# Moving one folded weight pair ahead of a branch, and its successor's loads behind a fetch

## The chip, the cores and the metric

The kernel runs on one core of one Trainium2 chip. The metric is the device time of one execution in microseconds (us). Three runs of the kernel before took 694.87, 694.79 and 693.70 us; their median is 694.79 us. Smaller is better. A separate execution was recorded by the hardware profiler; it took 693.57 us, and the span from its first to its last instruction, which all times below are counted from, is 691.8 us long.

The core has five engines that run their own instruction streams and wait for each other through semaphores: TensorE (PE in the profile, with weight loads shown apart as PEld), VectorE (DVE), ScalarE (ACT), GpSimd (POOL), and SyncE (SP), which here does nothing but start transfers.

## The reference, cut to what matters

The model is two transformer blocks on 800 tokens (8 sequences of 100) of width 512, all in float32:

```
x = x + attention0(layernorm(x), ctx[:, :100])     # 16 heads, causal
x = x + experts(layernorm(x))                      # 8 experts, 2 per token
x = x + attention1(layernorm(x), ctx)              # 16 latent heads over 361 rows
x = x + quantised_ffn(layernorm(x))                # 512 -> 2 x 1408 -> 512, int8-like rounding
```

Two parts touch the change. The first is the routing of the second line:

```
scores = x @ Wg.T ; topk_s, topk_i = top_k(scores, 2) ; probs = softmax(topk_s)
y += w[..., e] * (silu(x @ W1[e].T) * (x @ W2[e].T)) @ W3[e]     for each of 8 experts
```

The second is in the third line, where the queries of a head h pass through three weights one after the other:

```
q_hk = hidden_q @ Wq.T ; q_big = q_hk . w_kc_q[h] ; q_r = q_big . W_qr[h]
```

The product of those three weights doesn't depend on the data, so the kernel computes it once, two heads at a time, and multiplies the tokens with the result. That is called folding below, and two heads are a pair. There are eight pairs, 0 to 7.

## The kernel before, in words

The kernel goes through the four lines in order. Tokens are tiled in seven tiles of 128 rows (the last has 32). Each expert gets 240 slots in a DRAM buffer, `x_slot`: the routing computes for each token the slots of its two experts, and 14 indirect transfers started by POOL (line 680) scatter the normalised rows there. Expert e then fetches its 240 rows (`fetch`, line 960), turns them into columns by 8 transposes (`columns_of`, line 985; the two copies out of PSUM are lines 989 on ACT and 987 on DVE), and multiplies (`products`, line 1053).

**The branch.** Should an expert get more than 240 tokens, a slow path handles the rest. DVE computes a flag, `spilt` (line 806), PE, DVE, ACT and POOL each read it into a register (line 879), and all branch on it (line 886). The slow path isn't taken with these inputs, so each engine jumps over it. The rows of expert 0 can't be fetched before the scatters have landed, so around the branch PE has little else to do than folding.

**Folding a pair** takes a chain across two engines:

- `fold_head` (line 705): for each of the two heads three matmuls of 64 columns on PE; `fold_copy` (line 713): ACT copies the result to `a_p`. The two are `fold_first`.
- `fold_second` (line 723): two matmuls of 512 columns on PE, each on half of the array's columns; ACT copies the result to `f_p` (line 727).
- `fold_third` (line 733): four transposes on PE; ACT copies them into `wqf` (line 734), which the second attention reads much later.

A float32 matmul appears in the profile as two records, so the six matmuls of line 705 are x12 there.

A pair's weights are loaded by `fold_load` (lines 694, 698 and 699): five transfers started by SP, 1,088 KB together, into one of three buffers. Pairs 0 to 2 are loaded early. Pair 0 is folded ahead of the branch. Pairs 3 to 7 are folded one per expert, in experts 0 to 4, between the products of that expert (lines 1085, 1091 and 1103).

**The order of the work.** PE, DVE and ACT follow the order in which the code is written inside `tc.manual_schedule` regions; there is one up to line 868 and another from line 1035. Between them, and for SP's transfers, the framework's scheduler decides. `tc.issue_after` (line 1023) holds the transfers written behind it until the rows of expert 1 have been asked for. In the built program the first part of pair 1 stands wholly ahead of the branch on PE and ACT, both heads and the copy to `a_p`, although line 1037 is written behind it. Behind the branch stand, on PE, in this order: line 705 of pair 2, line 723 of pair 1, line 723 of pair 2, line 733 of pair 1, line 733 of pair 2, the transposes of expert 0's rows (line 985), and expert 0's products. On ACT stand a load of an activation table, `a_p` of pair 2, `f_p` of pairs 1 and 2, `wqf` of pairs 1 and 2, the rows' copy (line 989), and then the load of the table that holds Silu (line 1064). SP starts pair 3's five transfers ahead of the branch, and behind it the rows of experts 0 and 1, three tiles of `gu` (a weight of the last line that is quantised on the side, line 823), one of `dn` (line 828), and pair 4's five transfers.

## Time and profile before

| | |
|---|---|
| median of three runs | 694.79 us (693.70 to 694.87) |
| the profiled execution | 693.57 us, span 691.8 us |
| mean granted clock of TensorE over the span | 0.976 of full speed |
| PE busy | 651.2 us, 94% of the span |
| DVE, ACT, POOL busy | 419.9, 245.3, 183.6 us |
| longest idle time of PE around the branch | 8.12 us, until 136.12 us |
| expert 0's first product on PE | 145.71 us |
| last scatter started by POOL | 134.22 us |
| expert 0's rows asked for by SP | from 137.05 us |

How to read it: a row of an engine's timeline gives start, duration, engine, line and operation, with the tiles written and read, the number of records merged into it and, in brackets, how long that engine sat idle before it and what released it. The chain of work that ended last is followed back from the last instruction, so what stands on it set the end. PEclk is the share of full clock that the chip granted TensorE in a stretch. Idle time of an engine that isn't on the chain costs nothing.

### The profile page before, as it was taken

The numbers are of one execution on the slowest core, as the hardware profiler recorded it, in microseconds if no ns is written. First come the engines' busy times: TensorE is split into PE (matmuls) and PEld (weight loads), VectorE is DVE, ScalarE is ACT, GpSimd is POOL, SyncE is SP. The second block draws the span as 40 slices with busy tenths as digits, with TensorE's granted clock in tenths as the row PEclk, the third lists the DMA queues.
The fourth block names the chain that finished last, engine by engine and source line by source line (L and its number), as shares of the span: only waits on it lengthen the run. The fifth ranks groups of instructions, "written<-read, shape, count | busy, mean of one in ns | idle before, by whom it ended". The sixth has DMA issues, their size and how long they took to land.

```text
span 691.8 us, 10209 instructions
## 1 busy us (share of the span) xinstructions
PE 651.2 (94%) x3637; PEld 420.4 (61%) x3637; DVE 419.9 (61%) x1059; ACT 245.3 (35%) x557; POOL 183.6 (27%) x197
## 2 busy tenths in 40 slices
PE   8999997499999999996899999999999999999995
PEld 6767755466776677475676666666666644444442
DVE  4775688326666452442347867876666356566687
ACT  3554454141122111330135555555555412221140
POOL 2132231601111111168114233233333202211021
PEclk9999999589999999999799999999999999999999
DMA  8700293699999997744010210210000030111211
GB/s 296 236 17 18 95 328 114 238 306 260 308 275 311 315 254 186 191 137 133 15 16 1 57 42 16 57 34 11 2 12 1 3 125 8 29 28 29 48 35 63
DMA packets 80313, 80.41 MB, mean 116 GB/s; under 512 B 41284, under 2 KB 54136, under 8 KB 80128
## 3 DMA queue, kind: packets, MB, share of 16 engines
q1 hardware_dynamic: 76543, 70.97, 35.6%
q0 software_dynamic: 3712, 8.72, 5.6%
q8 instruction: 30, 0.49, 0.3%
q14 instruction: 28, 0.22, 0.1%
HBM read 56.36 MB, written 16.50 MB: 105 GB/s over the span
## 4 chain that ended last, share of the span: by engine, by line
PE 65%; DVE 7%; DMA 2%; POOL 2%; issue 2%; ACT 1%; SPq 1%; ACTq 0%; POOLq 0%; DVEq 0%
PE bank L357 11%; PE bank L1053 11%; PE bank L1330 10%; PE bank L1310 7%; PE bank L1267 6%; PE bank L1117 6%; PE bank L1324 4%; PE bank L1453 3%; POOL e L1318 2%; PE bank L1300 2%; PE bank L705 1%; DVE nm L1312 1%; PE bank L723 1%; PE bank L985 1%; DMA sin_sb<-in_rope_sin 1%
## 5 line engine op out<-in xcount | busy, mean ns | idle before, releaser
L1318 POOL TENSOR_SCALAR e<-e,rs 128x361 f32<-128x361 f32 (+1 forms) x56 | 66.9, 1196 | 146.4 <-DVE rs L1317 143.2
L357 PE MATMUL bank<-wvo,ctxT 128*128 128x512 f32 x192 | 83.9, 593 | 0.0
L1310 PE MATMUL bank<-kvT,qe 128*128 128x361 f32 (+1 forms) x208 | 82.0, 477 | 0.0
L1053 PE MATMUL bank<-xgT,w 128*128 128x240 f32 (+1 forms) x384 | 76.4, 370 | 0.9 <-ACT xgT L989 0.9
L1053 PEld LDWEIGHTS bank<-xgT,w 128*128 128x128 f32 (+1 forms) x384 | 63.9, 181 | 15.5 <-issue 9.9
L1330 PE MATMUL bank<-pT,kvr 121*128 121x400 f32 x192 | 70.4, 502 | 1.8 <-DVE pT L80 1.8
L1315 ACT ACTIVATE e<-bank,nm 128x361 f32<-128x361 f32 (+1 forms) x104 | 58.8, 565 | 31.3 <-DVE nm L1312 22.4
L1312 DVE TENSOR_REDUCE nm<-bank 128x1 f32<-128x361 f32 (+1 forms) x104 | 54.9, 528 | 21.5 <-PE bank L1310 20.4
L1324 PEld LDWEIGHTS bank<-ident,e 128*121 128x121 f32 (+1 forms) x312 | 47.3, 183 | 33.7 <-POOL e L1318 7.3
L357 PEld LDWEIGHTS bank<-wvo,ctxT 128*128 128x128 f32 x192 | 36.2, 190 | 43.1 <-issue 42.6
L1128 POOL DMA_INDIRECT x_acc<-y,place x16 | 24.4, 1526 | 125.4 <-ACT y L1127 122.1
L1324 PE MATMUL bank<-ident,e 128*121 128x128 f32 (+1 forms) x312 | 52.7, 279 | 2.1 <-POOL e L1318 2.1
L1470 POOL TENSOR_TENSOR hid<-g,u 128x512 f32<-128x512 f32 (+1 forms) x17 | 20.5, 1215 | 111.1 <-ACT g L1461 74.8
L1330 PEld LDWEIGHTS bank<-pT,kvr 121*128 121x128 f32 x192 | 33.9, 190 | 21.4 <-issue 2.0
L1267 PE MATMUL bank<-xT,wqf 128*128 128x256 f32 (+1 forms) x192 | 45.5, 399 | 0.7 <-ACT xT L1252 0.7
L322 POOL TENSOR_TENSOR s<-s,rs 100x800 f32<-100x800 f32 x16 | 24.4, 1523 | 72.4 <-DVE rs L321 30.5
L1117 PE MATMUL bank<-w,hT 128*128 128x512 f32 (+3 forms) x96 | 43.0, 596 | 0.3 <-DVE hT L1077 0.3
L1267 PEld LDWEIGHTS bank<-xT,wqf 128*128 128x128 f32 x192 | 37.4, 196 | 7.9 <-ACT xT L1252 0.9
L1310 PEld LDWEIGHTS bank<-kvT,qe 128*128 128x128 f32 (+1 forms) x208 | 32.5, 186 | 9.4
L82 ACT COPY pT<-bank 121x384 f32<-121x384 f32 (+1 forms) x51 | 23.8, 466 | 32.1 <-PE bank L1324 31.5
L80 DVE COPY ctxT<-bank 128x400 f32<-128x400 f32 (+2 forms) x23 | 13.1, 573 | 32.3 <-PE bank L1267 22.9
L1065 DVE TENSOR_TENSOR hT<-silu,bank 128x240 f32<-128x240 f32 x16 | 6.5, 404 | 39.5 <-ACT silu L1064 39.5
(251 smaller groups left out, 1034.6 us busy)
## 6 DMA issues: line engine op xcount, KB each, us to landing
w<-in_w SPq DMA_DIRECT2D x8, 1408.0 KB
gu<-in_wgu SPq DMA_DIRECT2D x22, 256.0 KB
w<-in_w SPq DMA_DIRECT2D x16, 256.0 KB
wq_p<-in_wq SPq DMA_DIRECT2D x8, 512.0 KB
wo<-in_wo SPq DMA_DIRECT2D x8, 512.0 KB
x_slot<-zeros SPq DMA_DIRECT2D x1, 3840.0 KB
kq_p<-in_wkcq SPq DMA_DIRECT2D x16, 192.0 KB
dn<-in_wdn SPq DMA_DIRECT2D x4, 704.0 KB
```

What stands on the lines that cost most here:

```text
L322: nc.gpsimd.tensor_tensor(part, part, rs.unsqueeze(2).to_broadcast([S, 8, S]), ALU.mult)
L357: nc.tensor.matmul(po[:, :D], lhs[:, c, ds(t * P, r)], rhs[:, c, :], start=(c == 0), stop=(c == chunks - 1),)
L1053: nc.tensor.matmul(po, w12_e[:, c, cols], xgT[:, c, :], start=(c == c0), stop=(c == c1 - 1))
L1117: nc.tensor.matmul(py[i][:n], hT[:mr, m, ds(s0, n)], w3_e[:mr, m, :], start=(m == 0), stop=(m == 2))
L1128: d = nc.gpsimd.indirect_dma_start(out=x_acc, out_offset=bass.IndirectOffsetOnAxis(ap=place[:, 0:1], axis=0), in_=y, in_offset=None, compu ...
L1267: nc.tensor.matmul(pq[:, i, :], wqf[:, c, ts(p0 + i, P)], xT[:, c, :], start=(c == 0), stop=(c == KC - 1),)
L1310: nc.tensor.matmul(ps[:r, :L], qe[:, ds(k0, r)], kvT, start=True, stop=True)
L1312: nc.vector.tensor_reduce(nm[:r], ps[:r, :L], AX.X, ALU.max, negate=True)
L1315: nc.scalar.activation(e[:r], ps[:r, :L], AF.Exp, bias=nm[:r], accum_out=sm[:r])
L1318: (nc.vector if odd else nc.gpsimd).tensor_scalar_mul(e[:r], e[:r], rs[:r])
L1324: nc.tensor.transpose(pt[:LP, c, :r], e[:r, ds(c * (LP - 1), LP)], ident[:r, :r])
L1330: nc.tensor.matmul(pc[:, :VC], kvr[:, c, :], pT[:, c, ts(j, VC)], start=(c == 0), stop=(c == LC - 1))
```

## The change

Four edits, all around the branch:

- Pair 1 is folded whole in the part written ahead of the branch: `fold_second` and `fold_third` of it now stand behind the matmuls that count each expert's tokens (line 800).
- Behind the branch only pair 2 is folded, step by step.
- A one-element Silu on ACT is written at the head of the second ordered region, so that the table with Silu is loaded there.
- Pair 3's loads move from ahead of the branch to behind the rows of experts 0 and 1, ahead of the `gu` tiles.

```diff
     part = fold_second(*part)
-    loaded.append(fold_load(pairs_left.pop(0)))
     xT = gate_columns(5, 7)
     fold_third(*part)
     gate_scores(5, 7, xT)
 
-    loads = loaded.pop(0)
-    pa = fold_head(*loads, 0)
+    part = fold_first(*loaded.pop(0))
     rank_choices(5, 7)
     give_slots(5, 7)
...
     spilt = gp.tile([P, 1], I32, tag="spilt", name="spilt")
     nc.vector.tensor_scalar(spilt, most, float(CAP), None, ALU.is_gt)
+    part = fold_second(*part)
+    fold_third(*part)
     close_atw()
...
     behind_slots = tc.issue_after(slots[1][-1][1])
     behind_slots.__enter__()
+    loaded.append(fold_load(pairs_left.pop(0)))
     gate_up_in = [load_gate_up(gate_up_left.pop(0)) for _ in range(GB)]
...
-    part = fold_copy(*loads, fold_head(*loads, 1, pa))
-    following = fold_first(*loaded.pop(0))
+    nc.scalar.activation(most, ln_eps, AF.Silu)
+    part = fold_first(*loaded.pop(0))
     part = fold_second(*part)
-    following = fold_second(*following)
     fold_third(*part)
-    fold_third(*following)
     turned = columns_of(0, slots[0])
```

In the built program the engines' orders change as follows. PE: line 723 and line 733 of pair 1 (six instructions) move from behind the branch to right ahead of PE's read of the flag. ACT: `f_p` and `wqf` of pair 1 move ahead of the branch too, and the scheduler puts the table load and the one-element Silu there as well, between them and ACT's read of the flag; the two table loads behind the branch are gone. DVE and POOL: no change of order. SP: pair 3's five transfers as said; expert 2's first weight load (line 483) now stands behind two transposing transfers and two loads that it stood ahead of, and the loads of the weights for the second attention (lines 1015 and 1018) stand later.

## The prediction

> **What bounds the kernel now.** I read the page first, then the chain of work that ended last around the branch, then the timelines of PE, ACT and SP there, and last a table of stretches. The page gives the span and the clock in 40 slices of 17.3 us:

> ```profile
> span 691.8 us, 10209 instructions
> ...
> PEclk9999999589999999999799999999999999999999
> ```

> PE is 94% busy, so time is lost only where PE waits or is slow. There are two dips of the clock; the first, in slices 7 and 8 (121 to 156 us), is where the change is. The chain of work from 126 to 150 us (start, duration, what):

> ```profile
> 131.97 4.14 issue
> 136.12 2.79 PE bank L705 x12
> 138.91 3.69 PE bank L723 x8
> ...
> 142.68 0.59 ACT f_p L727
> ...
> 144.57 0.59 ACT xgT L989
> ...
> 145.71 3.48 PE bank L1053 x16
> ```

> Behind the branch the end is set by PE's own folding, not by the rows: those of expert 0 landed at 139.68 and 141.31 us (completions of their semaphores), the transposes of line 985 start at 143.81. From 145.71 PE works through expert 0 without a gap. The change is worth what it moves that 145.71, and what it does to PE's speed behind it. ACT's timeline there:

> ```profile
> 138.99 1.28 ACT L713 ACT_TABLE_LOAD   x1 [11.32 <-PE bank L705]
> 140.28 0.27 ACT L713 COPY a_p<-bank 128x128 f32<-128x128 f32 x1
> 140.86 0.59 ACT L727 COPY f_p<-bank 128x512 f32<-128x512 f32 x1 [0.31 <-PE bank L723]
> ```

> The 1.28 us table load delays `a_p` of pair 2, but meanwhile PE runs line 723 of pair 1 (138.84 to 140.82): hidden. The stretches are cut where I found the clock to change (PE busy, PEld, DVE, ACT, POOL, PEclk, DMA share, GB/s):

> ```profile
> 2.69:6.11 3.42, 2.16 (x5) 0.78 (x4) 1.78 (x5) 0.29 (x1) 2.06 (x25) 1.00 0.91 270
> ...
> 118.74:122.16 3.42, 1.39 (x11) 1.11 (x12) 2.09 (x6) 2.68 (x5) 2.58 (x3) 1.00 0.81 218
> 122.16:125.57 3.41, 3.00 (x21) 2.07 (x19) 0.89 (x6) 0.94 (x3) 2.50 (x4) 0.50 1.05 375
> ...
> 135.81:139.23 3.42, 3.12 (x14) 2.93 (x16) 0.00 (x0) 0.24 (x1) 0.00 (x0) 0.50 0.36 92
> 139.23:142.64 3.41, 3.41 (x9) 0.43 (x6) 0.00 (x0) 1.90 (x3) 0.00 (x0) 0.50 0.97 268
> 142.64:146.05 3.41, 2.38 (x18) 1.95 (x19) 1.03 (x5) 3.18 (x5) 0.00 (x0) 1.00 1.01 374
> ...
> 333.78:337.20 3.42, 3.42 (x10) 2.75 (x9) 0.62 (x2) 0.29 (x2) 0.00 (x0) 0.50 0.02 5
> ```

> The clock falls to half at 122.16 and comes back at 142.64, after a stretch that PE filled with the four 512-wide matmuls of line 723. The stretch before, 91% busy with the 64-wide matmuls of line 705, didn't bring it back.

> [...] 122.16, 142.64, 326.96 and 337.20 are 6.0, 54.0 and 3.0 windows apart. [...] Here windows of 3.41 us out of 3.41 released it (139.23, 333.78, 6.11), windows of 3.12 and 3.00 didn't, nor did that from 2.69 with 2.16 (the 1.00 in its row is only the absence of an earlier record; its four matmuls of 384 columns take 2.93 us, half speed). [...] PE's second branch record takes 3.785 us (132.06 to 135.84).

> **The change part by part**, against the profiled execution (693.57 us, span 691.8), phase of the windows as there.

> *Pair 1 ahead of the branch.* It runs in PE's gap of 8.12 us, at half clock. Line 723 from 128.00, 1.98 us as measured behind the branch: 129.98. `f_p` 0.59 plus 0.05: 130.62. Line 733 from 130.70, about 1.1 us (four such transposes at half clock took 1.09 at 328.98): 131.8. PE's read of the flag stands behind it in order and could start at 130.54 before. It now has to follow the issue of line 733, some 0.45 us later; if the sequencer runs ahead of that wait, 0, at most 1.2 (to the end of line 733). I take 0.45, since PE also waits for its own last instruction (131.91 before) ahead of the jump. So PE comes out at 136.57 instead of 136.12: +0.45. POOL's scatters, DVE's flag and SP's fetch (137.05, released by the last scatter) don't wait for any of it.

> *Table load and Silu.* On ACT: `wqf` 131.9 to 132.5, table 1.28, the one element 0.2: 134.05. ACT waits for its own last instruction, then jumps. With PE's 3.8 us it is back at 137.9, before it is needed at 139.4 (end of line 705). Before, it jumped at 131.5 and gave no sign of life until 138.94, so its jump may take up to 7.4 us; that bound would cost 2.1 us. I take 0. The table load at 145.17, also taken away, was hidden by the first products (Silu at 149.23): 0.

> *Behind the branch, one pair.* Now nothing lies between the steps. Line 705: 136.57 + 2.79 = 139.36. `a_p` 0.27 and two hand-overs of 0.05: line 723 from 139.74, 1.98, to 141.72. `f_p`: line 733 from 142.42. The 1.98 and 0.66 us of pair 1 are gone from the chain, but PE stands still for 0.38 and 0.70 us, since no second pair fills those waits.

> *What that does to the clock.* The window 139.23 to 142.64 now holds 0.13 us of line 705, 1.98 of line 723 and 0.22 of line 733: 2.33 of 3.41, 68%, against 100%. The windows known to fail had 63% (from 2.69; 51% without transposes), 88% and 91%. So I take it that the clock doesn't come back. Then line 733 takes 1.1 (to 143.5), line 985 twice 0.98 (to 145.45), the second half's copy 0.2 + 0.62 as before (to 146.3), and the first product starts at 146.4: 0.7 later than 145.71. The window to 146.05 is transposes; the next, 146.05 to 149.47, is full of products, and releases the clock at 149.47. Until then a product record takes about 0.40 instead of 0.2175 us (3.48 for 16, times 1.83, as line 723's four records took 1.08 at full clock, at 117.25, and 1.98 at half): 3.07 us do the work of 1.67, a loss of 1.40. Sum: **+2.1 us**. If the window grid lies otherwise, the release comes up to one window later: another 3.41 x 0.456 = 1.6.

> *Pair 3's loads.* Five transfers, 1,088 KB. Pair 4's five took 3.9 us (147.6 to 151.5, semaphores). So everything behind them on SP's queue lands 3.9 us later, `gu` at 148.4 to 149.8 instead of 144.56 to 145.86, `dn` at 151.5 instead of 147.6. DVE takes the first `gu` at 149.95 and `dn` at 154.5: hidden, by 1.5 us at the least. Pair 3 itself lands at 147.4 and is wanted by PE at 149.0 (later with a slow clock): hidden by 1.6. If late, a us for each us. Expert 2's weights, asked for at 157.6, now wait for DVE's second `gu` (about 162); 1,408 KB at some 300 GB/s is 5 us more, needed at 182.3: hidden by over 10. The transfers removed from 116.9 to 119.9 freed bandwidth for the scatters, but POOL starts these 1.27 us apart and SP waits for the last start: 0.

> Sum +2.1 us on 693.57; the median of the runs shown is 1.2 above that execution, and I carry the difference over: 694.79 + 2.1 = 696.9 us. From no change this kernel's measurement can tell about 0.2%, 1.4 us.

> **The rivals.**
> *The clock comes back within the single pair's chain.* If a window needs only some 60% of matmuls, 142.64 stays the moment of release. Then line 733 ends at 143.2, line 985 at 144.2, the copy at 145.0, first product at 145.1: -0.6, so 694.2. It decides at a threshold under 68%; for: no window between 63% and 88% is in the trace; against: those of 88% and 91% failed, if on narrow matmuls. This one ends not slower.
> *The clock was late before, too, in most runs.* Only 3.74 us of line 723 stand there, a window is 3.41; if it must lie wholly inside, that happens for a tenth of the phases. Then the median of before is a slow-clock run: its first product comes at 147.4 (two pairs at half clock), after's at 146.4: -1.0 or, with an earlier window, up to -2.5; 693.8 to 692.3. For: two of three runs are 1.2 above the profiled one. Against: a loss of 3 us and more would show as a wider spread than 1.3.
> *ACT comes late out of the branch*, to 139.4 + 2.1: +2.1 on top of the first, 699.0. For: no record of ACT from 131.5 to 138.94. Against: PE's jump took 3.8.
> *The loads come late*: pair 3 by 1 us, +1 on top; 697.9. For: DMA share 1.0 from 138 on. Against: the slack of 1.6.

> **How the numbers follow.** Slow clock as worked out 0.52 (695.9 to 698.6 by the phase of the grid), ACT or loads late on top 0.12, clock back in the chain 0.20, clock late before 0.16. Likeliest 696.9. The range reaches from the clock rival, 693.9, to the latest release, 698.6; left out are the far ends of the last two. Slower by over 0.2% is the first two cases: 0.64. The clock rival is within 0.2% mostly: 0.21. Faster, mainly from the last: 0.15.

> **What would show it.** In the profile after: PE's line 723 twice, near 128 and 139.7; PE out of the branch near 136.6; idle pieces of PE of 0.4 and 0.7 us between lines 705, 723 and 733; first product near 146.4 with PEclk 0.50 until 149 to 153; no table load of ACT between 135 and 150; no wait of PE for `qr_p` or `kq_p`. A first product at about 145 with PEclk 1.00 makes me wrong, a first product past 147.5 would point at ACT or the loads.

## The result, and the profile after

The changed kernel takes 698.23 us (median of 13 runs, 694.93 to 699.97), the kernel before 694.87 us in the same measurement (13 runs, 692.44 to 697.12). The ratio is 1.0050 with a 95% interval of 1.0034 to 1.0067: slower by 3.4 us. The forecast was slower, by 2.1 us.

The profiled execution after took 696.34 us, 2.77 more than the one before. From its page:

```profile
span 694.6 us, 10206 instructions
...
PEclk9999999579999999999799999999999999999999
```

Slices 7 and 8 hold the first dip of the clock, now 5 and 7 where they were 5 and 8: the dip is longer. The second dip's 7 was there before. The chain of work that ended last, behind the branch (start, duration, what):

```profile
136.26 2.81 PE bank L705 x12
...
139.47 2.00 PE bank L723 x4
...
142.19 1.11 PE bank L733 x4
...
144.31 0.59 ACT xgT L989
...
145.81 4.96 PE bank L1052 x16
```

It goes through one pair now, step by step. PE's timeline adds, in brackets, PE's idle time ahead of each row and what ended it:

```profile
128.05 1.98 PE L723 MATMUL bank<-wq_p,a_p 128*64 128x512 f32 x4
130.71 1.12 PE L733 MATMUL bank<-ident,f_p 128*128 128x128 f32 x4 [0.69 <-ACT f_p L727]
136.26 2.80 PE L705 MATMUL bank<-qr_p,kq_p 128*128 128x64 f32 x12 [4.44 <-issue]
139.47 1.98 PE L723 MATMUL bank<-wq_p,a_p 128*64 128x512 f32 x4 [0.41 <-ACT a_p L713]
142.19 1.11 PE L733 MATMUL bank<-ident,f_p 128*128 128x128 f32 x4 [0.74 <-ACT f_p L727]
143.09 1.81 PE L985 MATMUL bank<-ident,xg 128*128 128x128 f32 x8
145.81 4.96 PE L1052 MATMUL bank<-xgT,w 128*128 128x240 f32 x16 [0.92 <-ACT xgT L989]
```

Pair 1 runs in the gap, at half clock (line 723's four records took 1.98 us). Behind the branch PE stands still three times. The first product comes at 145.81, as good as unmoved (145.71 before), but its sixteen records take 4.96 us instead of 3.48. The stretches, cut in steps of 3.41 us from the change of the clock at 121.51 (PE busy, PEld, DVE, ACT, POOL, PEclk, DMA share, GB/s), say why:

```profile
121.51:124.92 3.41, 2.89 (x18) 1.95 (x18) 0.47 (x3) 1.42 (x4) 2.80 (x3) 0.50 0.60 230
...
138.58:141.99 3.41, 2.45 (x7) 0.58 (x6) 0.00 (x0) 0.71 (x2) 0.00 (x0) 0.50 0.94 263
141.99:145.40 3.41, 2.71 (x12) 2.37 (x12) 0.31 (x1) 1.31 (x3) 0.00 (x0) 0.50 0.94 268
145.40:148.82 3.42, 3.00 (x8) 2.59 (x9) 1.00 (x7) 0.00 (x0) 0.00 (x0) 0.50 1.09 345
148.82:152.23 3.41, 3.41 (x24) 3.29 (x23) 1.00 (x2) 0.51 (x2) 0.00 (x0) 1.00 1.03 366
```

```profile
212.60 1.62 DVE L145 TENSOR_REDUCE amax<-dn 128x1 f32<-128x1408 f32 x1 [1.77 <-DMA dn<-in_wdn]
...
220.25 0.62 DVE L987 COPY xgT<-bank 128x448 f32<-128x448 f32 x1
```

```profile
220.97 3.48 PE L1052 MATMUL bank<-xgT,w 128*128 128x240 f32 x16 [0.67 <-issue]
```

The fourth `dn` tile landed at 212.57 us (205.12 before, where DVE took it at 209.16 without a wait). DVE follows the order of the code, so its copy of expert 4's rows came late: it ended at 220.87, 0.10 us before PE went on (`issue` in PE's bracket means that the view names no releaser).

Everything else is so regular that one table holds it. It is worked out from the starts of PE's records, for every profile of this study, in us. "Back" is from the last matmul of the counts (line 800 of the kernel before) to the first of line 705 behind the branch, "chain" from there to expert 0's first product, and the others from an expert's first product to the next one's.

| kernel | back | chain | expert 0 | 1 | 2 | 3 | 4 |
|---|---|---|---|---|---|---|---|
| before | 8.29 | 9.60 | 18.27 | 18.19 | 18.19 | 18.19 | 18.19 |
| before_again | 12.36 | 9.43 | 18.27 | 18.19 | 18.19 | 18.19 | 18.19 |
| silu_only | 8.40 | 9.62 | 18.27 | 18.19 | 18.19 | 18.19 | 18.19 |
| w2_late | 12.21 | 9.59 | 18.27 | 18.19 | 18.19 | 18.19 | 18.19 |
| loads_only | 11.75 | 9.60 | 18.26 | 18.19 | 18.19 | 18.19 | 18.19 |
| after | 8.31 | 9.55 | 19.75 | 18.19 | 18.19 | 19.02 | 18.26 |
| after_again | 9.94 | 9.55 | 20.75 | 18.19 | 18.19 | 18.19 | 18.19 |
| after_dn2 | 8.72 | 9.55 | 19.96 | 18.19 | 18.19 | 18.19 | 18.19 |
| after_w2 | 11.63 | 9.55 | 20.34 | 20.69 | 18.26 | 18.19 | 18.19 |
| fold_only | 12.03 | 9.55 | 20.06 | 18.19 | 18.19 | 18.19 | 18.19 |
| fold_filled | 12.16 | 8.42 | 18.27 | 18.19 | 18.19 | 18.19 | 18.19 |
| rows_first | 11.86 | 7.61 | 18.26 | 18.19 | 18.19 | 19.74 | 18.26 |
| best | 11.71 | 7.41 | 18.27 | 20.40 | 18.27 | 18.19 | 18.19 |
| rows_first_dn2 | 8.40 | 7.77 | 18.26 | 18.19 | 18.19 | 18.19 | 18.19 |

Between the profiles of before and after: ahead of the chain +0.14, chain -0.05, expert 0 +1.48, experts 3 and 4 +0.90, from expert 5 to PE's end +0.27; together 2.7 of the 2.8 us by which the spans differ.

### The profile page after: what moved, and what is told of

Same layout as the page of the kernel before. It is cut to its first block, busy times and chain, and to the rows that moved or that the text cites. A ratio compares the mean times of both kernels' runs of the same rounds, so it can differ in the third digit from the quotient of the medians.

```text
span 694.6 us, 10206 instructions
## 1 busy us (share of the span) xinstructions
PE 654.7 (94%) x3637; PEld 422.8 (61%) x3637; DVE 419.3 (60%) x1059; ACT 244.1 (35%) x557; POOL 183.6 (26%) x197
## 3 DMA queue, kind: packets, MB, share of 16 engines
q0 software_dynamic: 3712, 8.72, 5.4%
## 4 chain that ended last, share of the span: by engine, by line
PE 62%; DVE 7%; POOL 5%; DMA 3%; issue 2%; ACT 1%; SPq 1%; POOLq 0%; ACTq 0%; DVEq 0%
PE bank L357 11%; PE bank L1052 11%; PE bank L1329 9%; PE bank L1309 7%; PE bank L1116 6%; PE bank L1323 4%; PE bank L1266 3%; PE bank L1452 3%; POOL e L1317 2%; PE bank L1299 2%; PE bank L705 1%; DVE nm L1311 1%; PE bank L723 1%; PE bank L985 1%; POOL turned L1210 1%
## 5 line engine op out<-in xcount | busy, mean ns | idle before, releaser
L1052 PE MATMUL bank<-xgT,w 128*128 128x240 f32 (+1 forms) x384 | 77.9, 375 | 1.6 <-ACT xgT L989 0.9
L1311 DVE TENSOR_REDUCE nm<-bank 128x1 f32<-128x361 f32 (+1 forms) x104 | 54.9, 529 | 21.5 <-PE bank L1309 20.4
```

What stands on the lines that cost most here:

```text
L1052: nc.tensor.matmul(po, w12_e[:, c, cols], xgT[:, c, :], start=(c == c0), stop=(c == c1 - 1))
L1311: nc.vector.tensor_reduce(nm[:r], ps[:r, :L], AX.X, ALU.max, negate=True)
```

## The experiments

The theory after the result was that two things cost: the slow clock (expert 0) and the transfers (expert 3). Its rivals were that all of the loss is the one or the other. The measurements fall into four series, in which the kernel before took 694.87 (the result above), 698.35, 698.28 and 694.45 us; a time is compared with that of its own series. What differs in the middle two stands at the end.

**loads_only** and **fold_only** split the change. The first is the kernel before with this edit:

```diff
     part = fold_second(*part)
-    loaded.append(fold_load(pairs_left.pop(0)))
     xT = gate_columns(5, 7)
...
     behind_slots.__enter__()
+    loaded.append(fold_load(pairs_left.pop(0)))
     gate_up_in = [load_gate_up(gate_up_left.pop(0)) for _ in range(GB)]
```

The second is the changed kernel with the same edit turned back.

> The kernel before with one edit of the change alone: pair 3's five transfers move from ahead of the branch to behind the rows' transfers; folding, tables and the order on PE, DVE, ACT and POOL stay as before. The theory that the transfers cost (what the profiles differ by behind the first products, 2.82 less 1.58 us): slower by 0.7 to 1.8 us, the fourth down-projection tile lands about 7 us later than before (near 212 us), DVE waits for it, and PE stands idle for some 0.6 us ahead of expert 4's products; the first product stays near 145.7 and the clock comes back as before. The theory that the whole 3.4 us is the single pair's slow clock: 0, within 0.5 us of before.

> The changed kernel with pair 3's loads put back ahead of the branch; all else as changed (pair 1 whole ahead of the branch, one pair behind it, Silu's table first). If the loss is shared between clock and transfers: slower than before by 1.4 to 2.4 us; first product near 145.8 us, sixteen product records in 4.5 to 5.0 us against 3.48, PEclk 0.50 until 146 to 149; the fourth down-projection tile lands near 205 us, no wait of DVE for it. If all of the loss is the clock: slower by 3.0 to 3.6 us. If all of it is the transfers: 0, within 0.5 us.

loads_only: 698.61 us against 698.35, ratio 1.0015 (0.9997 to 1.0033), +1.0 us by the ratio (0.3 by the medians), with no change still inside the interval. fold_only: 700.93 us, ratio 1.0032 (1.0014 to 1.0050), +2.2 us. The sizes fit a shared loss (1.0 and 2.2 make 3.3), but only the larger part is clear of no change, and the interval of fold_only, up to 3.5 us, doesn't shut out that the clock is nearly all of it. In the profile of fold_only PE's timeline shows the slow products again:

```profile
144.09 1.97 PE L723 MATMUL bank<-wq_p,a_p 128*64 128x512 f32 x4 [0.41 <-ACT a_p L713]
146.80 1.11 PE L733 MATMUL bank<-ident,f_p 128*128 128x128 f32 x4 [0.74 <-ACT f_p L727]
...
150.43 5.28 PE L1052 MATMUL bank<-xgT,w 128*128 128x240 f32 x16 [0.92 <-ACT xgT L990]
```

The clock came back at 154.08, and expert 0 took 20.06. In loads_only, with two pairs behind the branch, it came back before the first product, and expert 0 took 18.26. But DVE's timeline of loads_only shows a wait that didn't reach PE in that execution (experts 3 and 4 took 18.19):

```profile
213.81 1.62 DVE L145 TENSOR_REDUCE amax<-dn 128x1 f32<-128x1408 f32 x1 [0.46 <-DMA dn<-in_wdn]
```

So the expectation of 0.6 us of idle PE failed for the profiled run: DVE's delay was too short to reach PE. Whether it does so in other executions, the traces don't show. An expectation of fold_only failed too. Its tile was to land near 205 us without a wait, but although its loads stand ahead of the branch as before, DVE waited there longer than in loads_only (PE again lost nothing):

```profile
216.40 1.62 DVE L145 TENSOR_REDUCE amax<-dn 128x1 f32<-128x1408 f32 x1 [0.64 <-DMA dn<-in_wdn]
```

So the two kernels split the times, but not the cause of the late tile: it comes with each half of the change alone.

**fold_filled** asks whether it is the idle pieces that keep the clock down. It is fold_only with matmuls that fill them and write a PSUM bank that nothing reads:

```diff
+    def filler(n, times=1):
+        pf = bank()
+        for _ in range(times):
+            nc.tensor.matmul(pf[:, :n], ident, xs[0][:, :n], start=True, stop=True)
...
     part = fold_first(*loaded.pop(0))
+    filler(112)
     part = fold_second(*part)
+    filler(208)
     fold_third(*part)
     turned = columns_of(0, slots[0])
+    filler(240)
```

> The kernel of the run fold_only with three more matmuls on PE (112, 208 and 240 columns of float32, into a PSUM bank that nothing reads), placed in PE's three idle pieces behind the branch: behind line 705, behind line 723 and behind the rows' transposes. The theory that the idle pieces keep the clock at half: in most executions it comes back one window of 3.41 us earlier, the first sixteen product records take 3.5 to 4.2 us, and 0.8 to 1.8 us of fold_only's loss is regained. The theory that the clock isn't ruled by those pieces (or that it takes wide matmuls throughout): same as fold_only or up to 0.4 us slower, since the fillers delay the chain a little.

698.29 us, ratio 1.0007 (0.9990 to 1.0024): 1.7 us regained by the ratios (1.0032 less 1.0007 of 698). The stretches of its profile, in the same columns:

```profile
140.75:144.16 3.41, 2.74 (x13) 2.77 (x14) 0.00 (x0) 0.00 (x0) 0.00 (x0) 0.50 0.31 87
144.16:147.58 3.42, 3.42 (x10) 1.30 (x10) 0.00 (x0) 0.85 (x2) 0.00 (x0) 0.50 0.93 266
```

and PE's timeline behind them:

```profile
147.94 0.98 PE L991 MATMUL bank<-ident,xg 128*128 128x128 f32 x8
148.76 0.58 PE L739 MATMUL bank<-x,ident 128*128 128x240 f32 x2
149.84 3.48 PE L1060 MATMUL bank<-xgT,w 128*128 128x240 f32 x16 [0.49 <-ACT xgT L995]
```

More work for PE, a chain 1.1 us shorter (8.42), and expert 0 at 18.27. The window that PE filled released the clock at 147.58, before the first product. The intervals of the two times still touch (1.0014 and 1.0024), but the profiles decide for the first cause: expert 0 took 18.26 or 18.27 in the four kernels of this study that put work into the pieces, and 19.75 or more in the five profiles without it. With the idle pieces of 0.4 and 0.7 us left open the clock came back 3.0 to 5.0 us behind the first product; with them filled here, 2.26 us ahead of it.

**rows_first** fills them with real work: in fold_only, the rows' transposes go ahead of pair 2's.

```diff
     part = fold_second(*part)
-    fold_third(*part)
     turned = columns_of(0, slots[0])
+    fold_third(*part)
```

> The kernel of the run fold_only with one swap behind the branch: the transposes of expert 0's rows stand ahead of pair 2's four transposes on PE (and the copy of the latter behind that of the rows on ACT). PE then has work in its wait for f_p and in its wait for the rows' copy. If the chain through the single pair sets the first product: it starts 1.0 to 1.5 us earlier than in fold_only (near 144.5 us), at half clock still, and the time falls by 0.7 to 1.5 us against fold_only. If the rows' landing (near 141.3 us) or the copies set it: 0 to 0.5 us.

696.94 us, ratio 0.9995 (0.9974 to 1.0016); 2.6 us below fold_only by the ratios, more than the 0.7 to 1.5 expected, because the clock came back too (at 144.37, first product 145.71), which no expectation had. The chain took 7.61. But of that, 1.55 was given back in expert 3 (19.74), by the wait that also stands in after:

```profile
211.72 1.62 DVE L145 TENSOR_REDUCE amax<-dn 128x1 f32<-128x1408 f32 x1 [2.48 <-DMA dn<-in_wdn]
```

Here, as in fold_only, pair 3's loads are ahead of the branch, so they can't be the only way to that wait.

**before_again**, **w2_late** and **after_w2** look for what makes the tile late. In all four kernels above the first transfer of expert 2's weights (1,408 KB) stands behind four transfers on SP's queue that it led in the kernel before. w2_late gives the kernel before that order (`gu_last` is the `gu` transfer asked for last; one load of a later pair moves up with it), after_w2 turns it round in the changed kernel.

```diff
         quantise_next()
-        if e + 2 < NE:
+        if e == 0:
+            with tc.issue_after(gu_last[0]):
+                experts[2] = load_expert(2)
+        elif e + 2 < NE:
             experts[e + 2] = load_expert(e + 2)
```

```diff
         if e < KC:
-            turn_down(*quantise_down(*down_in))
-            if e + 1 < KC:
-                down_in = load_down(e + 1)
+            dq = quantise_down(*down_in)
+        if 0 < e < KC:
+            turn_down(*dq)
+            if e + 1 < KC:
+                down_in = load_down(e + 1)
         gate_and_up(2)
+        if e == 0:
+            experts[2] = load_expert(2)
+            turn_down(*dq)
+            down_in = load_down(1)
         quantise_next()
```

> The kernel before, unchanged, for a second profile of it beside the next runs. In the four runs so far ACT copied pair 1's a_p at 129 to 132 us, 3 us or so after PE had finished it, where the first two profiles show no such gap (127.3 us); if that belongs to the place of the run and not to those kernels, it is here too, and PE comes out of the branch near 140 us; if it belongs to the kernels, a_p is at 127.3 us and PE out near 136 us.

> The kernel before with one edit: expert 2's first weight transfer (1,408 KB) is held until the second gu tile of expert 0 has been asked for, as it stands in the changed kernel and in all four runs so far; folding and pair 3's loads stay as before. If the place of that transfer on SP's queue is what makes the fourth dn tile late: slower by 0.7 to 1.8 us, expert 2's weights land 5 us or more later than before, the fourth dn tile 4 us or more later, and DVE waits for it. If pair 3's own transfers are needed for the delay: 0, within 0.5 us.

> The changed kernel with one edit: expert 2's four weight transfers go out ahead of the transposing transfer and load of the dn tile and of the second gu tile in expert 0; all else as changed, pair 3's loads behind the rows included. If their place on the queue is the cause of the later loss: 0.7 to 1.5 us faster than the changed kernel (ratio to before near 1.003 instead of 1.005), no wait of DVE for the fourth dn tile. If pair 3's transfers themselves are: as the changed kernel, 1.005.

before_again took 698.28 us, `a_p` was copied at 132.14 and PE was back at 141.23: the gap of ACT belongs to the place of the run, not to the kernels (more at the end). w2_late: 698.12 us against 698.28, ratio 0.9997 (0.9982 to 1.0012), no wait at the fourth tile (landed at 211.78, taken at 214.27). The later place of expert 2's weights doesn't by itself make the tile late. The test isn't clean, since the load that moved up with it (512 KB) stands behind the weights in the four kernels. after_w2 was slower instead of faster: 703.11 us (6 runs), ratio 1.0070 (1.0046 to 1.0094). The weights in front pushed the second `dn` tile back, and the same wait came two experts earlier (expert 1 20.69). DVE's timeline of after_w2:

```profile
180.34 1.62 DVE L145 TENSOR_REDUCE amax<-dn 128x1 f32<-128x1408 f32 x1 [3.44 <-DMA dn<-in_wdn]
```

There is one buffer for the tile (`bufs=1`), and its next transfer waits until DVE has quantised the one before; in this run, with expert 2's weights ahead of it on the queue, it was 3.44 us late for DVE.

**best** put rows_first, two fillers of 112 columns and after_w2's order together.

```diff
     part = fold_first(*loaded.pop(0))
+    filler(112)
     part = fold_second(*part)
     turned = columns_of(0, slots[0])
     fold_third(*part)
+    filler(112)
...
         gate_and_up(2)
+        if e == 0:
+            experts[2] = load_expert(2)
+            turn_down(*dq)
+            down_in = load_down(1)
```

> The kernel of the run rows_first (pair 1 ahead of the branch, pair 3's loads ahead of it too, the rows' transposes ahead of pair 2's) with two more edits: fillers of 112 columns on PE behind line 705 and behind pair 2's transposes (they write a PSUM bank that nothing reads), and expert 2's weights early on the queue as in the run after_w2. If the chain behind the branch, the clock and the queue are the three things that set the time here: 1.5 to 3 us faster than before, first product 7.4 to 7.7 us after PE is out of the branch (before: 9.6), clock back at or before it, no wait for the fourth dn tile. If the gain in front is given back behind, within 0.7 us of before.

698.94 us, ratio 1.0009 (0.9993 to 1.0025), not faster. The chain took 7.41, 2.0 us less than in before_again, and expert 1 took 20.40, 2.2 more: the gain was given back whole at the second `dn` tile.

**after_again** and **after_dn2** test that wait by taking away what makes it. after_dn2 is the changed kernel with two buffers and an earlier load:

```diff
-        w = qin.tile([P, NI], F32, tag="dn", name=f"dn{n}", bufs=1)
+        w = qin.tile([P, NI], F32, tag="dn", name=f"dn{n}", bufs=2)
...
-            turn_down(*quantise_down(*down_in))
-            if e + 1 < KC:
-                down_in = load_down(e + 1)
+            down_next = load_down(e + 1) if e + 1 < KC else None
+            turn_down(*quantise_down(*down_in))
+            down_in = down_next
```

> The changed kernel unchanged, beside the next runs. If its loss doesn't hang on the place of the run: ratio to before 1.0035 to 1.0065, as first measured (1.005). In the profile, with ACT's gap of some 4 us ahead of pair 1 as in the last eight profiles: PE out of the branch 11.6 to 12.4 us behind the counts, first product 9.5 us later, expert 0 taking 19.7 to 20.4 us from first product to the next expert's first product instead of 18.27.

> The changed kernel with one edit: two buffers for the dn tile, and each dn tile asked for ahead of the quantising of the one before it, so that its transfer no longer waits for DVE. The other engines' orders stay. If the late fourth dn tile is the second term of the loss: no wait of DVE for it, every expert from 1 to 5 takes 18.19 to 18.27 us, and it is 0.4 to 1.2 us faster than the changed kernel in the same job. If the transfers cost elsewhere, or nothing: within 0.4 us of the changed kernel.

after_again: 697.66 us against 694.45, ratio 1.0043 (1.0023 to 1.0063), the first result again; ACT's gap was not there this time, and PE was back after 9.94 us, with a branch record of 5.40. after_dn2: 696.75 us, ratio 1.0022 (1.0004 to 1.0040), 0.9 us below after_again by the medians, as expected in size; the intervals overlap, so the time alone doesn't prove it. In its profile no expert from 1 to 4 is longer than 18.19, and DVE doesn't wait (no bracket):

```profile
212.12 1.61 DVE L145 TENSOR_REDUCE amax<-dn 128x1 f32<-128x1408 f32 x1
```

In the profile of after_again DVE waited 0.63 us there, and PE lost nothing. So this term changes from execution to execution: 0.90 in one profile of the changed kernel, 0 in the other.

**silu_only** is the kernel before with the one-element Silu at the head of the second ordered region.

```diff
+    nc.scalar.activation(most, ln_eps, AF.Silu)
     part = fold_copy(*loads, fold_head(*loads, 1, pa))
```

> The kernel before with one edit: the one-element Silu, and with it the table load, comes first in the second ordered region; the scheduler puts both ahead of the branch on ACT, and the table loads ahead of a_p and of Silu behind the branch are gone. If the place of the table load costs nothing: within 0.5 us of before. If ACT's way through the branch became late by it: slower by up to 2 us, with PE waiting for a_p behind the branch.

694.80 us against 694.45, ratio 1.0004 (0.9986 to 1.0022), chain 9.62 against 9.60: nothing.

**rows_first_dn2** puts together what had helped: rows_first, two fillers of 112 columns, and the early `dn` tiles.

```diff
     part = fold_first(*loaded.pop(0))
+    filler(112)
     part = fold_second(*part)
     turned = columns_of(0, slots[0])
     fold_third(*part)
+    filler(112)
...
-            turn_down(*quantise_down(*down_in))
-            if e + 1 < KC:
-                down_in = load_down(e + 1)
+            down_next = load_down(e + 1) if e + 1 < KC else None
+            turn_down(*quantise_down(*down_in))
+            down_in = down_next
```

> The kernel of the run rows_first with the two fillers of 112 columns (written to a PSUM bank that nothing reads) and with the early dn tiles of the run after_dn2: pair 3's loads ahead of the branch, the rows' transposes ahead of pair 2's. If chain, clock and dn tile are what sets the time here: first product 7.4 us behind PE's return from the branch, 18.27 us for expert 0, no expert longer, and 1.5 to 3 us faster than before (ratio 0.9957 to 0.9978). If the gain is given back behind: within 0.7 us of before, and the table of experts shows where.

692.59 us (690.96 to 694.11, 22 runs) against 694.45, ratio 0.9975 (0.9963 to 0.9987): faster than both kernels, by 1.7 us than the one before and, by the medians, 5.1 than the changed one. PE's timeline behind the branch:

```profile
137.26 2.79 PE L705 MATMUL bank<-qr_p,kq_p 128*128 128x64 f32 x12 [4.53 <-issue]
139.84 0.71 PE L739 MATMUL bank<-x,ident 128*128 128x112 f32 x2
140.49 1.98 PE L723 MATMUL bank<-wq_p,a_p 128*64 128x512 f32 x4
142.39 1.72 PE L991 MATMUL bank<-ident,xg 128*128 128x128 f32 x8
143.95 0.60 PE L733 MATMUL bank<-ident,f_p 128*128 128x128 f32 x4
144.38 0.37 PE L739 MATMUL bank<-x,ident 128*128 128x112 f32 x2
145.03 3.48 PE L1059 MATMUL bank<-xgT,w 128*128 128x240 f32 x16 [0.27 <-issue]
```

Nothing but 0.27 us of idle time is left between the branch and the products; the chain takes 7.77 instead of 9.60 (1.83 less, close to the gain measured), the sixteen records take 3.48, and no expert is longer. The gain is shown by the 22 runs and not by this profile, which has the longest time of them: its counts came 1.0 us later than in before, its second dip of the clock lasted 13.65 us instead of 10.24, and its span, 692.4, is 0.6 longer. Moving pair 1 ahead of the branch pays with the idle pieces filled and the tile early; what the early tile alone would bring to the kernel before was not run.

## Why the prediction was right, and where it was not

**Pair 1 ahead of the branch (+0.45).** Times right: line 723 at 128.05 (forecast 128.00), `f_p` at 130.07 to 130.65, line 733 at 130.71. The 0.45 didn't come: 8.31 us from the counts to line 705, 8.29 before. The trace shows PE's read of the flag starting at 130.71, with line 733's issue, and PE's branch record from 132.05 on, before and after alike (132.06). The lower end of the bound, 0, was the value.

**The table (0).** Right, twice. ACT's timeline of after shows the load and then a copy that waited for PE, not for the table, and silu_only measured 1.0004:

```profile
132.47 1.28 ACT L1038 ACT_TABLE_LOAD   x1
133.76 0.20 ACT L1038 ACTIVATE most<-ln_eps 128x1 f32<-128x1 f32 x1
139.15 0.27 ACT L713 COPY a_p<-bank 128x128 f32<-128x128 f32 x1 [5.19 <-PE bank L705]
```

ACT's second branch record starts at 134.06, 0.10 us behind the end of that Silu. The rival of ACT being late out of the branch is out with it.

**One pair behind the branch.** The idle pieces are 0.41 and 0.74 us (forecast 0.38 and 0.70), lines 723 and 733 at 139.47 and 142.19 (139.74 and 142.42, the difference is mostly the 0.45 less the 0.14 us by which this execution stood later at line 705).

**The clock (+0.7 and +1.40).** The course was right: the window from 138.58 was 72% busy (68%), the clock came back at 148.82 (149.47). The chain's +0.7 was too much; it is +0.10 in these executions. Besides the 0.45, the transposes of line 985 were counted as 1.96 us and took 1.81, and the next line starts some 0.2 us before the recorded end of the last one (line 985 at 143.09, line 733 until 143.30). The loss in the products was too little: 1.48 in this execution, but 1.48, 1.69, 1.79, 2.07 and 2.48 in the five profiles of kernels with one unfilled pair (table, less 18.27), 1.90 in the mean. The clock came back 3.0, 3.5, 3.7, 4.2 and 5.0 us behind the first product in those; I had taken the phase of the one trace for the middle, and it was the early end. That the two errors nearly cancel is luck: 2.1 forecast, 1.9 by these profiles, 2.2 (1.0 to 3.5) by fold_only's time.

**Clock late before, too; clock back in the chain.** Both fell: expert 0 took 18.26 or 18.27 in five of five profiles with two pairs behind the branch, and never less than 19.75 in the five with one that nothing fills.

**Pair 3's loads (0).** This is the step that failed: a term put at 0 where PE lost 0.90 us in the profile. Each slack that it names held: `gu`, pair 3 and expert 2's weights (172.85 us, 7.9 later, wanted past 182) cost nothing. What it left out is the fourth `dn` tile. The stretches of the kernel before, and then of the changed one (the last two columns are DMA share and GB/s):

```profile
116.00:126.00 10.00, 6.79 (x44) 4.56 (x43) 5.77 (x25) 5.17 (x9) 6.73 (x7) 0.81 0.72 233
...
148.00:212.00 64.00, 64.00 (x318) 46.00 (x317) 40.79 (x98) 12.76 (x28) 9.23 (x6) 1.00 1.08 286
```

```profile
116.00:126.00 10.00, 6.78 (x42) 4.55 (x41) 5.50 (x24) 5.17 (x9) 6.90 (x7) 0.78 0.47 177
...
148.00:212.00 64.00, 64.00 (x314) 46.55 (x313) 38.15 (x94) 12.74 (x28) 9.23 (x6) 0.99 1.12 281
```

The change takes transfers from a stretch with room (the share falls from 0.72 to 0.47) and puts them into one that shows a share of 1.08 to 1.12 for 64 us. At the fourth `dn` tile, whose slack was 4.04 us, there was still a delay: it was asked for 4.80 us later and was 2.65 longer on its way. Of these 7.45 us the slack and the products' own delay (1.58 by then) cover 5.6; DVE waits 1.77, PE loses 0.90. That the delay lasted because the stretch had no room is my estimate from those shares. I had priced each transfer against its next user, and not followed the queue to its tightest one. By the times this term is 0.9 (after_again less after_dn2) or 1.0 (loads_only), neither beyond doubt.

Nor do the moved loads alone own it. Counted from expert 1's first product, DVE is ready for the tile after 45.2 us where it needn't wait. It landed after 41.1, 42.8, 43.0 and 42.7 us in before, silu_only, before_again and w2_late; after 45.7 in loads_only, 45.9 in fold_only, 47.0 in after and 47.7 in rows_first. So, in one profile each, moving the loads makes it late, and so does the rest of the change with the loads left in place. Why, and why the tile was longer on its way, stays open.

**The sum.** +2.1 forecast, +3.4 measured (+3.2 in after_again): fold and clock 2.2, the late tile some 1.0 as far as the times tell. The likeliest case, its course and its sign were right. What came on top is nearest to the case "loads late", which had a share of the 0.12, but at another tile than it named.

## What to carry to other kernels

Work that fills another step's wait may be worth more than its own time: the two interleaved pairs kept PE busy for 3.41 of 3.41 us (139.23 to 142.64), and with one taken away the clock came back at 148.82 instead of 142.64 though the chain got no longer (9.55 us against 9.60). So move such work only together with something that fills the waits it leaves, real work first. And where a queue has as little room as here (a DMA share of 1.08 and 1.12 over 64 us), price a change against the tightest consumer on it, not only the next one; here the tile was late even in kernels that left the loads where they were.

## What the runs showed of the hardware

**Behind which windows the clock came back.** Three windows, of before, after_again and rows_first, have about the same busy time; the first is shown in the prediction (135.81 to 139.23, 3.12 us busy), the others are

```profile
137.49:140.90 3.41, 3.00 (x13) 1.98 (x12) 0.00 (x0) 0.27 (x1) 0.00 (x0) 0.50 0.79 226
```

```profile
140.96:144.37 3.41, 3.06 (x10) 1.45 (x11) 0.00 (x0) 0.85 (x2) 0.00 (x0) 0.50 0.94 267
```

Of the three only the last released the clock (at 144.37). After's window of products, with 3.00 us busy (145.40 to 148.82), released it too. The first two are mostly matmuls of 64 columns (line 705: 2.79 of 3.12 us and 1.87 of 3.00); the last is 1.97 us of 512-column matmuls and otherwise 128-column transposes. In rows_first_dn2 the window from 140.40 to 143.82 was filled (3.42 us busy), 40% of it with transposes, and released too. After's window from 138.58 had the same 1.98 us of line 723, 0.48 of line 705 and no transposes, and behind it the clock was still 0.50; so it was behind a window of transposes alone, 79% busy (141.99). My estimate from these seven windows is that transposes counted as a part of a well filled window, and that the narrow matmuls of line 705 counted less, if at all; no run sets the two apart.

**ACT stood still ahead of the branch on some chips.** In all eight profiles of the two slower series (recorded on chips 3 and 0) ACT started a copy 2 to 4 us after PE had finished what it needed. ACT's timeline of before_again (PE's line 705 ended at 128.2 there):

```profile
124.33 0.29 ACT L596 COPY parts<-bank 128x160 f32<-128x160 f32 x1
132.14 0.27 ACT L713 COPY a_p<-bank 128x128 f32<-128x128 f32 x1 [7.51 <-remote]
```

In the other profiles that have the same order (five of six; silu_only has another) it started within 0.1 us. In these eight PE is back from the branch after 11.6 to 12.4 us instead of 8.3 to 9.9, and in their series the kernel before takes 698.3 instead of 694.5 to 694.9 us. It comes with the place of the run and not with an edit, since the unchanged kernel shows it in before_again and not in before. The cause stays open.

**The taken branch.** PE's branch record took 3.65 to 5.40 us over fourteen profiles (3.79 before, 3.95 after), whatever stood ahead of it. In both, transfers of instructions start inside it (at 132.91 and 132.64 us); for which engine isn't recorded.
